# The last batch's row scatters bound to other steps of the routing

## The chip, the cores and the metric

The kernel runs on one core of a Trainium2 chip. The metric is the device time of one execution in microseconds. The reader needs these engines: TensorE (PE, matrix products; PEld is its weight load), VectorE (DVE), ScalarE (ACT), GpSimd (POOL) and SyncE (SP). DMAs are issued by SP and, where rows go to computed places ("indirect" DMAs), by POOL; all of them run on the core's 16 DMA engines. An instruction starts when its engine has reached it and every semaphore it waits for has its value.

## The reference, cut to what matters

Four batches of 512 tokens with 256 features go through two layers. Each layer is an attention followed by a mixture of experts, and everything is float32. The change touches only the experts of the second layer:

```python
logits = xf @ Wg                                   # 8 experts
top_vals, top_idx = jax.lax.top_k(logits, 2)
gate_score = jax.nn.softmax(top_vals, axis=-1)
comb = jnp.einsum('tke,tk->te', one_hot, gate_score) * alpha
for e in range(8):
    hdn = _layernorm(xf, ln_w[e], ln_b[e])
    a = jax.nn.gelu(hdn @ fc1_w[e] + fc1_b[e], approximate=True)
    y = a @ fc2_w[e] + fc2_b[e]
    out = out + y * comb[:, e:e + 1]
```

Each of the 2048 tokens needs only two of the eight experts, so the kernel sorts the tokens by expert and computes only those products.

## The kernel before, in words

**Sorting by scatter.** `route_steps` handles one batch of 512 tokens: it normalizes, computes the logits, picks two experts for each token and counts places. The result is `rt_posi` (line 931), the row in the DRAM buffer `rows` for each of a token's two copies. Eight indirect DMAs on POOL per batch (line 951, 128 rows of 258 floats each) write the normalized tokens from `rowbuf` to those places. They are put into a list, `pending`. `scatter_pending(n, behind)` takes the next n from that list and records them; if `behind` is given, the DMA also waits for that instruction. The reason given in the code is that the DMAs are to come a few at a time beside the other work.

**The last batch.** Its routing cannot lie beside attention, since attention is over by then. `layer1_attention` ends with a loop over `PIECES` in which the steps of this routing alternate with pieces of four expert tiles that were started ahead (`y_ahead`, `hp_ahead`; two tiles each of experts 0 and 1, whose rows were already there). The order in this stretch is:

- the places of the last batch, `rt_posi`; the first two of its eight scatters follow without any other wait;
- `tile_table` on DVE (lines 1009 to 1068): from the counts it works out for each of 39 tiles which expert and which rows it has. Its first large step is a comparison that makes `tt_past` (line 1025); the table that SP reads is `tab`, whose third row is finished at line 1047 (`L1.tabled`); `tt_valid` and `tt_aside` follow;
- two additions of the second biases to x (line 998, `L1.biased`), after which the batch's x is written to `out` by SP (line 1000).

In the kernel before, the third and fourth scatter wait for `L1.tabled`, the fifth and sixth for the first bias addition, the seventh and eighth for the second.

**What waits for the scatters.** `layer1_experts` then runs the expert tiles. SP loads the 128 rows of the first three tiles (line 1215, `row<-rows`). The first of these loads waits for all scatters, since a tile's rows may come from any of them. PE turns a tile's rows (line 1120, `ht`), multiplies with the first weights (line 1145, `hp`) and the second (line 1170, `y`). POOL adds the result to `out` with an accumulating indirect DMA (line 1188), one at a time. Of the four tiles ahead, the fourth's `y_ahead` stands behind the first tile's `ht` in PE's order.

**What sets the order.** PE's order and, among the experts, SP's order are written out by hand. DVE, ACT and POOL are ordered by a scheduler. Its order of DVE, ACT and POOL instructions, and the order on PE and SP, are the same in both kernels; only waits of POOL instructions differ.

Of the kernel before, what the change touches and what calls it, by code (L numbers as in the profile page):

```python
# [13 lines left out]
ALU = mybir.AluOpType  # L14
# [21 lines left out]
TILES = NB * S * 2 // P + EX - 1  # L36
GROUP = 32
RING = 3
# [25 lines left out]
def two_layers(ctx: ExitStack, tc: tile.TileContext, io, out):  # L64
    nc = tc.nc
# [616 lines left out]
    def layer1_attention(sts):  # L682

        units = []
        for b in range(NB):
            units += [(b, t, n) for t in range(NT) for n in range(NC)]
        ps, aTs = {}, {}
        routes, queries = {}, None  # L690
        kvs = mha_kvs(sts, (NB - 1,))
        done = None
        for i in range(len(units) + 4):
            if i < len(units):
                b, t, n = units[i]
                ps[i] = mha_scores(sts[b], n, t)
                unit = sts[b]
                if i + 1 < len(units) and units[i + 1][0] > 0 and units[i + 1][2] == 0:
                    bias = mha_bias(sts[units[i + 1][0]], units[i + 1][1])
                    after(bias, done, "a piece to a unit")  # L700
                done = sts[b]["unit"]
            if i < 3:
                next(kvs)
            if 0 <= i - 2 < len(units):
                b, t, n = units[i - 2]
                turns = mha_turns(sts[b], n, t, ps[i - 2][0])
                aTs[i - 2] = next(turns)
                next(turns)
            if 11 <= i < 15:
                next(kvs)  # L710
            if 0 <= i - 4 < len(units):
                b, t, n = units[i - 4]
                if n == NC - 1:
                    added = mha_out(sts[b], t)
            if 0 <= i - 3 < len(units):
                b, t, n = units[i - 3]
                mha_values(sts[b], n, t, aTs.pop(i - 3), ps.pop(i - 3)[1])
            for route in routes.values():
                next(route, None)
            if pending and (i < len(units) or i % 2 == 1):  # L720
                scatter_pending(2, unit["unit"] if i < len(units) else added)
            if i == 2:
                next(kvs)
            if queries:
                next(queries, None)
            if 0 <= i - 2 < len(units):
                next(turns)
            b = i // (2 * NT) + 1
            if b < NB and i % (2 * NT) == QUERIES:
                queries = mha_q_pieces(b, sts)  # L730
            if i == len(units) - 5:
                slots = slots_ahead()
            if i == len(units) - 3:
                held = []
                tiles = tiles_ahead(slots, *load_ahead(), sts[NB - 1]["unit"], held)
            if i == len(units) + 2:
                next(tiles)
            b, k = divmod(i - 11, 2 * NT)
            if k == 0 and 0 <= b < NB:
                routes[b] = route_steps(L1, b)  # L740
                next(routes[b])
        scatter_pending(2, L1.normed)
        for n in PIECES:
            for _ in range(n):
                next(tiles, None)
            for route in routes.values():
                next(route, None)
            if len(L1.run) < NB:
                scatter_pending(2, L1.turned)
            if len(L1.run) == NB and L1.table is None:  # L750
                L1.table = tile_table(L1)
                scatter_pending(2, L1.tabled)
        for i in L1.biased:
            scatter_pending(2, i)
        for _ in range(LEFT):
            next(tiles)

        for add in held:
            add()
        held.clear()  # L760
        return slots, tiles, held
# [53 lines left out]
    L1 = Layer(1, EX, FF1 // P, ET0, None)  # L815
# [188 lines left out]
    def tile_table(L):  # L1004

        lim = L.run[NB - 1][:, 0:EX]
        big_shape = [P, TILES, EX]
        n = tsmall([P, EX], "tt_n")
        i = nc.vector.tensor_tensor(n, lim, base[:, 0:EX], ALU.subtract)
        after(i, L.placed, "the rows' places first")  # L1010
        if L.done is not None:
            nc.vector.tensor_tensor(n, n, L.done[:, 0:EX], ALU.subtract)
        nc.vector.tensor_scalar(n, n, float(P - 1), None, ALU.add)
        n_i = tsmall([P, EX], "tt_ni", I32)
        nc.vector.tensor_copy(n_i, n)
        nc.vector.tensor_scalar(n_i, n_i, 7, None, ALU.logical_shift_right)
        nt = tsmall([P, EX], "tt_nt")
        nc.vector.tensor_copy(nt, n_i)

        c = tsmall([P, EX], "tt_c")  # L1020
        nc.vector.tensor_copy(c[:, 0:1], nt[:, 0:1])
        for e in range(1, EX):
            nc.vector.tensor_tensor(c[:, e : e + 1], c[:, e - 1 : e], nt[:, e : e + 1], ALU.add)
        past = t4(big_shape, f"tt_past{L.n}")
        nc.vector.tensor_tensor(
            past, c.unsqueeze(1).to_broadcast(big_shape), tile_f.unsqueeze(2).to_broadcast(big_shape), ALU.is_le
        )
        ef = const.tile([P, TILES], F32, tag="tt_ef", name=f"tt_ef{L.n}")
        nc.vector.tensor_reduce(ef, past, AX.X, ALU.add)
        nc.vector.tensor_scalar(ef, ef, float(EX - 1), None, ALU.min)  # L1030
        step = tsmall([P, EX], "tt_step")
        nc.vector.tensor_scalar(step, nt, float(-P), float(REGION), ALU.mult, ALU.add)
        if L.done is not None:
            nc.vector.tensor_tensor(step, step, L.done[:, 0:EX], ALU.subtract)
            nc.vector.tensor_tensor(step, step, L.done[:, 1:], ALU.add)
        tmp = t4(big_shape, f"tt_tmp{L.n}")
        nc.vector.tensor_tensor(tmp, past, step.unsqueeze(1).to_broadcast(big_shape), ALU.mult)
        off = const.tile([P, TILES], F32, tag="tt_off", name=f"tt_off{L.n}")
        nc.vector.tensor_reduce(off, tmp, AX.X, ALU.add)
        nc.vector.scalar_tensor_tensor(off, tile_f, float(P), off, ALU.mult, ALU.add)  # L1040
        if L.done is not None:
            nc.vector.tensor_scalar(off, off, L.done[:, 0:1], None, ALU.add)
        tab = const.tile([P, 3, TILES], I32, tag="tab", name=f"tab{L.n}")
        nc.vector.tensor_copy(tab[:, 0, :], ef)
        nc.vector.tensor_scalar(tab[:, 1, :], off, float(EX * REGION - P), None, ALU.min)
        nc.vector.tensor_tensor(tab[:, 2, 0:RING], ef[:, 0:RING], L.held, ALU.not_equal)
        L.tabled = nc.vector.tensor_tensor(tab[:, 2, RING:], ef[:, RING:], ef[:, 0 : TILES - RING], ALU.not_equal)

        dl = tsmall([P, EX], "tt_dl")
        i = nc.vector.tensor_tensor(dl[:, 0 : EX - 1], lim[:, 1:], lim[:, 0 : EX - 1], ALU.subtract)  # L1050
        after(i, L.placed, "the rows' places first")
        i = nc.vector.tensor_scalar(dl[:, EX - 1 :], lim[:, EX - 1 :], -1.0, None, ALU.mult)
        after(i, L.placed, "the rows' places first")
        nc.vector.tensor_tensor(tmp, past, dl.unsqueeze(1).to_broadcast(big_shape), ALU.mult)
        left = const.tile([P, TILES], F32, tag="tt_left", name=f"tt_left{L.n}")
        nc.vector.tensor_reduce(left, tmp, AX.X, ALU.add)
        nc.vector.tensor_tensor(left, left, off, ALU.subtract)
        nc.vector.tensor_scalar(left, left, lim[:, 0:1], None, ALU.add)
        valid = const.tile([P, TILES], F32, tag="tt_valid", name=f"tt_valid{L.n}")
        nc.vector.tensor_scalar(valid, left, token[:, 0:1], None, ALU.is_gt)  # L1060
        aside = const.tile([P, TILES], F32, tag="tt_aside", name=f"tt_aside{L.n}")
        if L.n == 0:
            past_ys = float(2 * NB * S)
            nc.vector.tensor_scalar(aside, valid, -past_ys, past_ys, ALU.mult, ALU.add)
        else:
            nc.vector.tensor_scalar(aside, valid, spare_neg, spare, ALU.mult, ALU.add)
        total = const.tile([1, 1], I32, tag="tt_total", name=f"tt_total{L.n}")
        nc.vector.tensor_copy(total, c[0:1, EX - 1 :])
        return tab, valid, aside, total
# [408 lines left out]
```

## Time and profile before

| | |
|---|---|
| three runs, us | 915.99, 918.59, 918.94 (median 918.59) |
| profiled execution, us | 917.38 |
| its span, us | 915.6 |
| granted TensorE clock | 0.996 of full |
| PE busy | 868.2 us (95%) |
| DVE busy | 426.1 us (47%) |
| ACT busy | 334.2 us (36%) |
| POOL busy | 226.2 us (25%) |
| scatters (line 951) | 64, min 967 ns, median 973, max 1394 |
| mean DMA rate | 155 GB/s |

The span is the time between the first and last recorded instruction; 1.78 us of the profiled execution lie outside it. Busy times are sums over the whole span. A POOL span of an indirect DMA is the time in which POOL works on the instruction, not the time in which the data move. In the timeline a line has the start and the duration in us, the engine, the source line, the operation with its output and inputs, and in brackets how long the engine sat idle before and what it waited for. "SPq" is SP's issue of a DMA. Starts are in us from the beginning of the span.

### The profile page before, as it was taken

How to read it: one execution, taken by the hardware profiler on the slowest of the kernel's cores; microseconds unless marked ns; L12 is line 12 of the kernel's file. 1: busy time of each engine (PE TensorE's matmuls, PEld its weight loads, DVE VectorE, ACT ScalarE, POOL GpSimd, SP SyncE). 2: the span in 40 equal slices, each digit the busy share in tenths (PEclk: the TensorE clock that was granted, in tenths of full speed). 3: DMA queues.
4: the chain of work that ended last, by engine and by line, in shares of the span. 5: the costliest groups of instructions: out<-in, count | busy, mean ns of one | idle time of the engine just before them, and what ended most of it. 6: DMA issues, size and time to landing. Idle time of an engine off the chain costs nothing.

```text
span 915.6 us, 15375 instructions
## 1 busy us (share of the span) xinstructions
PE 868.2 (95%) x5578; PEld 659.9 (72%) x5578; DVE 426.1 (47%) x1253; ACT 334.2 (36%) x749; POOL 226.2 (25%) x276
## 2 busy tenths in 40 slices
PE   6899999998999998999999999999989999999995
PEld 2456464755699996556676666667879999999995
DVE  5646473736623331765675686676721111111120
ACT  4323331222211111475574565565512333222231
POOL 2303014044313222000130250351642122122122
PEclk9999999999999999999999999999999999999999
DMA  8999933030188893600000123221257956877961
GB/s 309 293 261 245 246 134 112 15 101 35 54 276 262 252 347 116 229 24 1 24 2 1 46 69 119 71 70 56 74 158 247 304 168 193 262 238 239 322 213 22
DMA packets 55028, 142.08 MB, mean 155 GB/s; under 512 B 6894, under 2 KB 32933, under 8 KB 48800
## 3 DMA queue, kind: packets, MB, share of 16 engines
q1 hardware_dynamic: 39264, 102.89, 33.5%
q0 software_dynamic: 15392, 38.10, 16.4%
q8 instruction: 48, 0.79, 0.3%
q14 instruction: 36, 0.29, 0.1%
q10 hardware_dynamic: 288, 0.00, 0.0%
HBM read 131.52 MB, written 39.91 MB: 187 GB/s over the span
## 4 chain that ended last, share of the span: by engine, by line
PE 43%; DVE 7%; issue 4%; ACT 4%; DMA 2%; POOL 0%; SPq 0%; POOLq 0%; ACTq 0%; DVEq 0%
PE hp L1145 12%; PE y L1170 11%; PE s L616 5%; PE a2t L639 4%; PE o L664 4%; ACT p L629 2%; DVE p L625 2%; PE q L600 1%; ACT a2T L644 1%; PE hp_ahead L1145 1%; PE ht L1120 1%; PE wo L679 1%; DMA ys<-yw,to 1%; PE o L670 1%; DMA yb<-ys 1%
## 5 line engine op out<-in xcount | busy, mean ns | idle before, releaser
L1154 ACT ACTIVATE aT<-hp,w1s 128x128 f32<-128x128 f32 x248 | 67.3, 382 | 163.3 <-issue 153.2
L1145 PEld LDWEIGHTS hp<-hT,w1s 128*128 128x128 f32 x992 | 115.8, 192 | 2.4 <-DVE hT L1126 0.8
L1145 PE MATMUL hp<-hT,w1s 128*128 128x128 f32 x992 | 116.1, 275 | 0.6 <-DVE hT L1126 0.6
L1170 PE MATMUL y<-w2s,aT 128*128 128x256 f32 x496 | 112.3, 379 | 0.5 <-ACT aT L1154 0.5
L1170 PEld LDWEIGHTS y<-w2s,aT 128*128 128x128 f32 x496 | 91.8, 190 | 11.9 <-ACT aT L1154 0.7
L629 ACT ACTIVATE p<-p,s_nm 128x1024 f32<-128x1024 f32 x64 | 73.5, 1148 | 73.3 <-DVE s_nm L625 73.2
L625 DVE CUSTOM_DVE_ANT_0 p<-s,mbias 128x1024 f32<-128x1024 f32 x64 | 75.7, 1221 | 38.7 <-PE s L616 38.6
L1188 POOL DMA_INDIRECT out<-yw,to x31 | 47.8, 1541 | 168.1 <-DMA out<-yw,to 59.6
L1174 DVE TENSOR_SCALAR yw<-y,row 128x256 f32<-128x256 f32 x59 | 28.6, 484 | 122.3 <-PE y L1170 122.3
L951 POOL DMA_INDIRECT rows<-rowbuf,rt_posi x64 | 64.2, 1004 | 81.8 <-DVE rt_posi L931 25.4
L639 PEld LDWEIGHTS a2t<-ident,p 128*128 128x128 f32 x512 | 56.2, 142 | 36.8 <-issue 21.7
L639 PE MATMUL a2t<-ident,p 128*128 128x128 f32 x512 | 70.8, 278 | 5.7 <-DVE xn2T L594 2.6
L616 PE MATMUL s<-kT,q2T 64*128 64x512 f32 x256 | 65.1, 615 | 0.7 <-DVE s_nm L625 0.7
L664 PE MATMUL o<-a2T,v 128*64 128x128 f32 x1024 | 63.3, 276 | 0.1
L315 PE MATMUL s<-ctxT,q0T 128*128 128x512 f32 x128 | 62.4, 634 | 0.7 <-ACT q0T L292 0.7
L664 PEld LDWEIGHTS o<-a2T,v 128*64 128x64 f32 x1024 | 55.4, 137 | 8.5 <-issue 6.8
L644 ACT COPY a2T<-a2t 128x512 f32<-128x512 f32 x96 | 53.3, 582 | 16.1 <-PE a2t L639 16.1
L1126 DVE TENSOR_SCALAR hT<-ht,w1s 128x128 f32<-128x128 f32 x62 | 22.6, 406 | 77.3 <-PE ht L1120 71.2
L345 PE MATMUL hq<-a0T,ctxn 128*128 128x512 f32 x128 | 56.8, 596 | 0.1
L1145 PEld LDWEIGHTS hp<-hT,w0s 128*128 128x128 f32 x448 | 54.3, 192 | 3.2 <-DVE hT L1122 1.8
L1145 PE MATMUL hp<-hT,w0s 128*128 128x128 f32 x448 | 55.0, 276 | 1.0 <-DVE hT L1122 1.0
L1170 PE MATMUL y<-w0s,aT 128*128 128x256 f32 x224 | 53.1, 380 | 0.7 <-ACT aT L1150 0.7
(258 smaller groups left out, 1206.8 us busy)
## 6 DMA issues: line engine op xcount, KB each, us to landing
w1s<-in_w1p SPq DMA_DIRECT2D x34, 1030.0 KB
w2s<-in_w2p SPq DMA_DIRECT2D x34, 1024.0 KB
rows<-zeros POOLq DMA_DIRECT2D x8, 2064.0 KB
w0s<-in_w1p SPq DMA_DIRECT2D x31, 512.0 KB
w0s<-in_w2p SPq DMA_DIRECT2D x31, 512.0 KB
row<-rows SPq DMA_DIRECT2D x59, 129.0 KB
ctxT<-in_ctxT SPq DMA_DIRECT2D x4, 1024.0 KB
ctxn<-in_ctx SPq DMA_DIRECT2D x4, 1024.0 KB
```

The costliest lines, as they stand in the source:

```text
L315: nc.tensor.matmul(sp[:, h, :], st["qT"][:, c, bass.ts(t, P)], ctxT[b][:, c, bass.ts(h, 512)], start=(c == 0), stop=(c == NC - 1),)
L345: nc.tensor.matmul(op, ctxn[b][:, j, bass.ts(c, P)], aT[:, j, :], start=(j == 0), stop=(j == NJ - 1))
L616: nc.tensor.matmul(sps[r][:, k, :], st["qT"][at, n, bass.ts(t, P)], st["kT"][at, n, bass.ts(k, 512)], start=True, stop=True,)
L625: nc.vector.tensor_tensor_reduce(p, sps[r].rearrange("p h n -> p (h n)"), st["mbias"][:, t, :], -ATT_SCALE, -ATT_SCALE * LEAST, ALU.add, A ...
L629: nc.scalar.activation(p, p, AF.Exp, bias=nm, scale=-1.0, accum_out=tot[:, r : r + 1])
L639: nc.tensor.transpose(pt[:, bass.ts(j, P)], p[:, bass.ts(4 * g + j, P)], ident)
L644: nc.scalar.copy(d, pt)
L664: nc.tensor.matmul(op[r * HD : r * HD + HD, :], st["v"][:, j, bass.ts(2 * n + r, HD)], aT[:, r, bass.ts(j, P)], start=(j == 0), stop=(j == ...
L951: i = nc.gpsimd.indirect_dma_start(out=rows[:, :], out_offset=bass.IndirectOffsetOnAxis(ap=pos_i[:, k, t : t + 1], axis=0), in_=buf[:, k, ...
L1145: nc.tensor.matmul(o, w1[:, c * ff + f * P : c * ff + f * P + P], hT[:, c, :], start=(c == 0), stop=(c == NC - 1),)
L1154: nc.scalar.activation(aT[:, f, :], hp[:, f // 4, bass.ts(f % 4, P)], AF.Gelu_apprx_tanh, bias=w1[:, at : at + 1])
L1170: nc.tensor.matmul(op, aT[:, f, :], w2[:, f * D : f * D + D], start=(f == 0), stop=(f == nf - 1))
```

## The change

The third and fourth scatter of the last batch now wait for the comparison that makes `tt_past`, the fifth and sixth for the end of `tab`, the seventh and eighth for the first bias addition. The first two are as they were. No instruction is added, removed or put elsewhere in an engine's order. The diff:

```diff
@@ layer1_attention @@
             if len(L1.run) == NB and L1.table is None:
                 L1.table = tile_table(L1)
-                scatter_pending(2, L1.tabled)
-        for i in L1.biased:
-            scatter_pending(2, i)
+                for i in L1.tabled:
+                    scatter_pending(2, i)
+        scatter_pending(2, L1.biased[0])
         for _ in range(LEFT):
             next(tiles)
@@ tile_table @@
         past = t4(big_shape, f"tt_past{L.n}")
-        nc.vector.tensor_tensor(
+        begun = nc.vector.tensor_tensor(
             past, c.unsqueeze(1).to_broadcast(big_shape), tile_f.unsqueeze(2).to_broadcast(big_shape), ALU.is_le
         )
@@
-        L.tabled = nc.vector.tensor_tensor(tab[:, 2, RING:], ef[:, RING:], ef[:, 0 : TILES - RING], ALU.not_equal)
+        done = nc.vector.tensor_tensor(tab[:, 2, RING:], ef[:, RING:], ef[:, 0 : TILES - RING], ALU.not_equal)
+        L.tabled = begun, done
```

## The prediction

> **What bounds the kernel now.** I read the page's busy times first: PE is busy in 868.2 of 915.6 us, so a change that touches no product can gain only where PE stands still. Then I read the waits of PE from 675 us to the end, to see what the experts' stage loses: there are three, `ht` on the DMA of `row` (2.6 us, once), `hp` on DVE's `hT` (0.6) and the last `y` on ACT (0.5). After the first of these the chain of waits consists of PE's `hp`, `ht` and `y` alone up to 887 us. So there is one gap that this change can reach, and what fills it comes off the end. The timeline around it:
>
> ```profile
> 657.80 0.16 DVE L931 CAST rt_posi<-rt_pos 128x8 int32<-128x8 f32 x1
> ...
> 658.74 0.97 POOL L951 DMA_INDIRECT rows<-rowbuf,rt_posi  x1 [2.09 <-issue]
> ...
> 660.01 0.97 POOL L951 DMA_INDIRECT rows<-rowbuf,rt_posi  x1 [0.30 <-DVE tt_step L1034]
> ...
> 661.01 0.48 DVE L1025 TENSOR_TENSOR tt_past<-tt_c,tile_f 128x312 f32<-128x312 f32 x1
> ...
> 663.38 0.19 DVE L1047 TENSOR_TENSOR tab<-tt_ef 128x36 int32<-128x36 f32 x1
> ...
> 664.35 0.97 POOL L951 DMA_INDIRECT rows<-rowbuf,rt_posi  x1 [3.36 <-issue]
> ...
> 665.62 0.97 POOL L951 DMA_INDIRECT rows<-rowbuf,rt_posi  x1 [0.30 <-DVE tt_left L1058]
> 665.75 0.68 DVE L998 TENSOR_TENSOR x<-b,x 128x512 f32<-128x512 f32 x1
> ...
> 667.21 0.97 POOL L951 DMA_INDIRECT rows<-rowbuf,rt_posi  x1 [0.61 <-issue]
> ...
> 668.48 0.97 POOL L951 DMA_INDIRECT rows<-rowbuf,rt_posi  x1 [0.30 <-issue]
> 669.76 0.97 POOL L951 DMA_INDIRECT rows<-rowbuf,rt_posi  x1 [0.30 <-issue]
> ...
> 671.03 0.97 POOL L951 DMA_INDIRECT rows<-rowbuf,rt_posi  x1 [0.30 <-issue]
> ...
> 674.41 2.13 SPq L1215 DMA_DIRECT2D row<-rows  x3
> ...
> 676.38 0.44 PE L1120 MATMUL ht<-ident,row 128*128 128x128 f32 x2 [2.58 <-DMA row<-rows]
> ```
>
> Eight scatters, each 0.97 us long, follow each other at 1.27 us where nothing holds them. POOL stands idle for 3.36 us before the third and 0.61 before the fifth. The eighth starts at 671.03; SP, which has waited for it 5.1 us by its own list of waits, issues the first row load 3.38 us later; PE starts `ht` 1.97 us after that. PE's last product ahead of `ht` starts at 670.19 and lasts 3.62, so PE is free at 673.81: it waits 2.58 us for rows. That makes the scatters' end the wait that ends last here.
>
> **The new starts.** Three scatters of before give the time from the end of the DVE step that is waited for to the scatter: 657.96 to 658.74, 663.57 to 664.35 and 666.43 to 667.21, each 0.78 us. With this and the pitch of 1.27:
> - First and second: 658.74 and 660.01, as now.
> - Third: the comparison at line 1025 ends at 661.49, plus 0.78 is 662.27. Fourth: 663.54.
> - Fifth: line 1047 ends at 663.57, which would allow 664.35, but POOL is free only at 664.81. Sixth: 666.08.
> - Seventh: the first bias addition ends at 666.43, which would allow 667.21; POOL gives 667.35. Eighth: 668.62.
>
> So the eighth starts 671.03 - 668.62 = 2.41 us earlier. Only the first of the three waits binds: from the third on the scatters are back to back. The same lags of 3.38 and 1.97 us put the row load at 672.00 and the rows at 673.97, 0.16 us after PE is free. Of the gap of 2.58 us 2.41 go, and late next is PE itself, whose end at 673.81 caps the gain at 2.58.
>
> **What takes some of it back.** The batch's x (512 KB) is written to `out` from 667.34 on, and in the table of stretches the DMA engines are full in 669 to 670:
>
> ```profile
> 668.00:669.00 1.00, 1.00 (x12) 1.00 (x11) 0.00 (x0) 0.00 (x0) 0.70 (x2) 1.00 0.69 245
> 669.00:670.00 1.00, 1.00 (x12) 1.00 (x11) 0.00 (x0) 0.00 (x0) 0.69 (x2) 1.00 1.02 346
> 670.00:671.00 1.00, 1.00 (x8) 0.92 (x7) 0.00 (x0) 0.00 (x0) 0.73 (x1) 1.00 0.60 198
> 671.00:672.00 1.00, 1.00 (x7) 0.87 (x6) 0.00 (x0) 0.38 (x2) 0.96 (x1) 1.00 0.37 132
> ```
>
> The last two columns are the DMA engines' share and the rate in GB/s. A scatter alone moves 132 KB at 132 GB/s and a share of 0.37, as the last one did. Now the last one's data fall into the full microsecond. Its delay is at least nothing (the engines have room again from 670) and at most about the half microsecond in which the write of x uses what is left of the engines; I take 0.2, nearer to nothing, because before the sixth scatter ran through the same stretch and the seventh and eighth were not held up. Net gain 2.4 - 0.2 = **2.2 us**.
>
> **What else moves, at no cost.** Behind the scatters in POOL's queue stands only the first addition to `out` (672.31 before, 669.9 at the earliest now); it must also wait for the write of x, and the next additions follow it one by one. Nobody waits for them soon: POOL is idle for 8.8 us before the fourth. If this addition meets the row loads, it did so before. SP runs its table reads and weight loads behind the row loads, so these come 2.4 us earlier with PE. The tile that needs new weights (its loads were issued at 681.09 and 681.78, the DMA engines then full to 689) has its `hT` ready at 691.65 for an `hp` at 692.07: 0.4 us of room. As PE and SP both move with the rows, that room stays; should it go, it costs some tenths. The last 30 us (branch, last tile, last addition) follow PE and move as a whole.
>
> [...] The third to sixth scatter now run while DVE is fully busy (busy 2.60 of 2.60 us from 662.20 on) with the table, where before POOL was idle. [...] The row first: all 64 scatters of this trace last between 967 and 1394 ns. The best row is the same table in the first layer, beside eight scatters back to back:
>
> ```profile
> 238.53 0.98 POOL L951 DMA_INDIRECT rows<-rowbuf,rt_posi  x1 [0.30 <-issue]
> 239.81 0.97 POOL L951 DMA_INDIRECT rows<-rowbuf,rt_posi  x1 [0.30 <-issue]
> 241.09 0.97 POOL L951 DMA_INDIRECT rows<-rowbuf,rt_posi  x1 [0.30 <-issue]
> ```
>
> There the comparison, its reductions and products last 0.47 to 0.48 us each, as they do without scatters in the second layer. Neither engine holds the other up, so by the rows the price is nothing. [...]
>
> **Sum.** The profiled execution took 917.38 us: a span of 915.6 and 1.78 around it. 917.38 - 2.2 = **915.2**. The three runs' median is 918.59, from which the same gain would give 916.4. About 0.3% (2.75 us) is what a measurement of this kernel can tell from no change: my gain is 0.24% and its cap 0.28%, so it lies just inside that bound, and the runs' own spread of 2.95 us decides on which side it is read.
>
> **The rivals.**
> 1. *The gain stands, at its full size or a bit more.* The row loads come at the cap of 2.58 us or the downstream loads fall better: 914.8, and against the median of the runs shown over 0.3%. For it: the gap's size and PE as the only bound after it. Against: the tenths lost to the write of x.
> 2. *Hidden anyway.* The rows come earlier, but another wait ends at the same place: the row loads meet the first addition to `out`, or the weights of the tile at 692 come late. Price 1.5 to 2.5 us of the gain, leaving about 917. For it: the full DMA engines from 682 to 689 and the 0.4 us of room. Against: both loads move with PE.
> [...]
> 4. *The change doesn't do what it says*, if POOL waits for later DVE steps than named. The waits are counts of DVE's instructions, and the three lags of 0.78 us show that such a wait is released by the step named. I give it little, within the second case.
>
> **How the numbers follow.** My forecast of 915.2 (own range 914.8 to 915.7) has 0.54, the first rival 0.15, the second with the fourth 0.14, the third with the page's price 0.17. Half of the forecast's weight, less a little, and nearly all of the first rival's are read as more than 0.3% faster: 0.42. The rest of the forecast and the second give 0.40 for no change. The slower cases, most of which lie over 0.3%, and a little for what I do not see give 0.18. The range of 912.8 to 919.5 holds forecast, first and second rival with the runs' spread around them, and leaves out most of the third.
>
> **What would show it.** Right: scatters 3 to 8 of the last batch back to back at 1.27 us, the last 2.4 us nearer to `rt_posi`; their duration still 0.97; table steps of 0.48 us; SP's wait for the scatters shorter by 2.2 to 2.4 us; PE's wait before the first `ht` down from 2.58 to 0.4 us or less. Wrong: scatters longer than 1.4 us, gaps in DVE's table, `hp_ahead` later than 8.7 us after `rt_posi`, a row load that lands later than 2 us after its issue, or a new wait of `hp` after 676 us.

## The result, and the profile after

The changed kernel takes **915.10 us** (median of 20 runs, 913.38 to 917.41) against 917.68 us (20 runs, 915.82 to 919.77) of the kernel before, taken in turn on the same chip. The ratio is 0.9976, with a 95% interval of 0.9969 to 0.9983: 2.2 us faster by the ratio, 2.6 by the medians. The profiled execution took 914.52 us with a span of 912.7 and a mean granted clock of 0.993 (before 917.38, 915.6 and 0.996).

The timeline of the changed kernel around the change. Lines from 1048 on carry a number one higher than before:

```profile
656.10 0.17 DVE L931 CAST rt_posi<-rt_pos 128x8 int32<-128x8 f32 x1
...
657.03 0.97 POOL L951 DMA_INDIRECT rows<-rowbuf,rt_posi  x1 [2.10 <-issue]
658.30 0.98 POOL L951 DMA_INDIRECT rows<-rowbuf,rt_posi  x1 [0.30 <-DVE tt_c L1023]
...
659.31 0.48 DVE L1025 TENSOR_TENSOR tt_past<-tt_c,tile_f 128x312 f32<-128x312 f32 x1
...
660.57 0.98 POOL L951 DMA_INDIRECT rows<-rowbuf,rt_posi  x1 [1.28 <-issue]
...
661.85 1.25 POOL L951 DMA_INDIRECT rows<-rowbuf,rt_posi  x1 [0.30 <-DVE tt_off L1040]
...
662.17 0.24 DVE L1042 TENSOR_SCALAR tt_off<-tt_off,done 128x39 f32<-128x39 f32 x1
...
662.71 0.40 DVE L1045 TENSOR_SCALAR tab<-tt_off 128x39 int32<-128x39 f32 x1
...
663.41 0.97 POOL L951 DMA_INDIRECT rows<-rowbuf,rt_posi  x1 [0.30 <-DVE tt_left L1058]
...
664.68 0.97 POOL L951 DMA_INDIRECT rows<-rowbuf,rt_posi  x1 [0.31 <-issue]
...
664.81 5.47 PE L1146 MATMUL hp_ahead<-hT_ahead,w1s 128*128 128x128 f32 x32
...
665.96 0.97 POOL L951 DMA_INDIRECT rows<-rowbuf,rt_posi  x1 [0.30 <-issue]
667.24 0.97 POOL L951 DMA_INDIRECT rows<-rowbuf,rt_posi  x1 [0.30 <-issue]
...
670.12 3.62 PE L1171 MATMUL y_ahead<-w2s,aT_ahead 128*128 128x256 f32 x16
...
670.51 2.33 SPq L1216 DMA_DIRECT2D row<-rows  x3
...
673.57 0.38 PE L1121 MATMUL ht<-ident,row 128*128 128x128 f32 x2
```

The two profiles are best laid over each other at the start of `rt_posi` (657.80 before, 656.10 after):

| us after `rt_posi` starts | before | after | moved |
|---|---|---|---|
| third scatter | 6.55 | 4.47 | 2.08 earlier |
| eighth scatter | 13.23 | 11.14 | 2.09 earlier |
| first row load issued | 16.61 | 14.41 | 2.20 earlier |
| `hp_ahead` starts | 8.71 | 8.71 | 0 |
| PE starts `ht` | 18.58 | 17.47 | 1.11 earlier |

PE starts `ht` without a wait; the list of PE's waits from 650 to 900 us, in which before had 2.6 us for `row`, now begins with these (total, times, longest):

```profile
PE hp L1146 <- DVE hT L1127: 0.6, 1, 0.6
PE y L1171 <- ACT aT L1155: 0.5, 1, 0.5
PE b L994 <- DVE yw_ahead L1175: 0.2, 1, 0.2
```

So of the 2.86 us between the two profiled executions, 1.11 arise in the stretch of the change. Another 1.70 is the distance between the two `rt_posi`; nothing is changed ahead of it, and it is already there at 380 us. That part is scatter between executions. The 1.11 are fewer than the 2.20 that the rows gained, because `hp_ahead` took 5.47 us in place of 3.84. The table of stretches of the changed kernel says why. Its columns are the length of the slice, the busy time and the instructions of PE, PEld, DVE, ACT and POOL, then the granted PE clock, the DMA engines' share and GB/s:

```profile
665.00:666.00 1.00, 1.00 (x6) 1.00 (x6) 0.61 (x1) 0.00 (x0) 0.69 (x2) 0.50 0.30 103
666.00:667.00 1.00, 1.00 (x7) 1.00 (x7) 0.00 (x0) 0.00 (x0) 0.94 (x1) 0.50 0.74 243
667.00:668.00 1.00, 1.00 (x6) 1.00 (x6) 0.00 (x0) 0.00 (x0) 0.76 (x1) 0.50 0.99 345
668.00:669.00 1.00, 1.00 (x10) 1.00 (x8) 0.00 (x0) 0.00 (x0) 0.21 (x1) 0.80 0.74 250
669.00:670.00 1.00, 1.00 (x11) 1.00 (x10) 0.00 (x0) 0.00 (x0) 0.39 (x1) 1.00 0.24 83
```

The reader is to see the clock column at 0.50 for three slices, with six or seven products a microsecond where the last slice, at full clock, has eleven. No such stretch was in the profile of before at this place, so the first question was whether the change made it.

### The profile page after: what moved, and what is told of

Its sections match the earlier page's. It is cut to its first block, busy times and chain, and to the rows that moved or that the text cites. A ratio compares the mean times of both kernels' runs of the same rounds, so it can differ in the third digit from the quotient of the medians.

```text
span 912.7 us, 15375 instructions
## 1 busy us (share of the span) xinstructions
PE 868.7 (95%) x5578; PEld 662.3 (73%) x5578; DVE 426.4 (47%) x1253; ACT 334.3 (37%) x749; POOL 226.4 (25%) x276
## 4 chain that ended last, share of the span: by engine, by line
PE 45%; DVE 6%; ACT 4%; issue 4%; POOL 0%; ACTq 0%; POOLq 0%; DVEq 0%
PE hp L1146 12%; PE y L1171 11%; PE s L616 5%; PE a2t L639 4%; PE o L664 4%; ACT p L629 2%; DVE p L625 2%; PE hp_ahead L1146 1%; PE q L600 1%; PE v L510 1%; ACT a2T L644 1%; PE k L496 1%; PE y_ahead L1171 1%; PE ht L1121 1%; PE wo L679 1%
```

## The experiments

The kernels ran in three sets; those of a set and their runs of before share a chip. "Clock" is the mean over a kernel's runs of each run's mean granted TensorE clock.

| kernel | set | runs | median, us | ratio to before [95%] | clock |
|---|---|---|---|---|---|
| before again | 1 | 22 | 917.67 | 1.0002 [0.9994, 1.001] | 0.9927 |
| after again | 1 | 6 | 914.81 | 0.9961 [0.9945, 0.9976] | 0.9948 |
| no waits | 1 | 6 | 921.42 | 1.004 [1.0026, 1.0055] | 0.9905 |
| all late | 1 | 6 | 922.48 | 1.0051 [1.0035, 1.0067] | 0.9907 |
| first wait undone | 2 | 22 | 916.44 | 0.9988 [0.9977, 0.9999] | 0.9935 |
| first wait alone | 2 | 14 | 916.91 | 1.0006 [0.9991, 1.002] | 0.9935 |
| six at `tt_past` | 2 | 18 | 914.17 | 0.9967 [0.9956, 0.9978] | 0.9949 |
| four at once | 2 | 6 | 912.27 | 0.9946 [0.9927, 0.9965] | 0.9963 |
| after, third time | 3 | 12 | 915.24 | 0.9984 [0.9969, 0.9998] | 0.9947 |
| four at once again | 3 | 12 | 919.55 | 1.003 [1.0014, 1.0046] | 0.9922 |
| six at once | 3 | 8 | 920.53 | 1.0034 [1.0015, 1.0053] | 0.9916 |
| four, then at `tt_past` | 3 | 6 | 921.16 | 1.0058 [1.0039, 1.0078] | 0.9915 |

The runs of before had medians of 917.39, 916.89 and 916.69 us and clocks of 0.9929, 0.9936 and 0.9940 in the three sets. The ratio is not the quotient of the two medians; the two differ by up to 0.0011 ("after again" has 0.9972 by its medians), which is not small against the effects here. In every experiment each engine's instructions stand in the order of the changed kernel; only waits of scatters differ.

### Both kernels once more

No edit. Before:

> The kernel before, unchanged, to see each run's mean granted TensorE clock. In the profile of the changed kernel that clock was halved for 3.8 us within the stretch of the change (665 to 668.8), and its runs show mean clocks of 0.992 to 0.995. Theory A (the halving has nothing to do with the change; the old gap of 2.58 us hid its 1.6 us): the runs of before show the same mix, most at 0.993 to 0.994 and some at 0.995 to 0.996, and time does not depend on which. Theory B (the change brings the halving about): before is at 0.995 to 0.996 in all runs. Median 917.7 us, ratio 1.000 within 0.001.

After:

> The changed kernel, unchanged, on the same chip. Both theories: 915.2 us, ratio 0.9975. Theory A: runs at the higher clock are faster than those at the lower one by 1.1 to 1.3 us, since PE's end now decides when the first tile's rows are turned. In the profile the eighth scatter starts 11.1 us after the places (13.2 before).

The gain repeats (0.9961), and the profile of the changed kernel has the slow `hp_ahead` again (5.47 us, clock at 0.5 from 666.0 to 669.4). But the profile of before has a slow stretch too, in another place, in PE's timeline right behind the gap:

```profile
676.34 0.69 PE L1120 MATMUL ht<-ident,row 128*128 128x128 f32 x2 [2.90 <-DMA row<-rows]
676.82 4.79 PE L1170 MATMUL y_ahead<-w2s,aT_ahead 128*128 128x256 f32 x16
```

`y_ahead` took 4.79 us where it took 3.62 in the first profile of before: the clock was halved from 675.8 to 679.2. Half-clock stretches thus come without the change too, in some executions and not in others of the same kernel. This one costs 1.2 us (4.79 - 3.62), the one in `hp_ahead` 1.6 (5.47 - 3.84); each is 3.4 us long, not the 3.8 that the expectation read.

### All later

```diff
-                for i in L1.tabled:
-                    scatter_pending(2, i)
-        scatter_pending(2, L1.biased[0])
+        scatter_pending(6, L1.biased[1])
```

> The last six scatters wait for the second bias addition: the third starts at 10.3 us after the places, the eighth at 16.6, which is 3.4 us later than before. Theory (each microsecond of the last scatter is one of the end while PE waits): 917.7 + 3.4 = 921.1 us, ratio 1.0037, and PE's wait for the first rows 6.0 us, or 4.4 with the halved clock, at the same time. Rival (the gap was not what set the end): ratio below 1.002.

The sign and the size of the lever are confirmed: the eighth scatter starts 16.69 us after `rt_posi`, 3.46 later than before, and PE's wait in the timeline grows to 4.52:

```profile
679.75 0.69 PE L1119 MATMUL ht<-ident,row 128*128 128x128 f32 x2 [4.52 <-DMA row<-rows]
680.23 5.55 PE L1169 MATMUL y_ahead<-w2s,aT_ahead 128*128 128x256 f32 x16
```

The ratio (1.0051) is above the expected 1.0037: `y_ahead` pays 1.93 us more behind the longer gap, with the clock at a half from 677.3 to 684.1. This run also answers the question about `hp_ahead`. Its scatters come later than before, and `hp_ahead` still takes 5.47 us, with the clock at a half from 667.1 to 670.5: the slow `hp_ahead` does not need earlier scatters. PE's long wait hides that loss here.

### Which of the three waits carries the gain

The first wait undone, the other two as changed:

```diff
-                for i in L1.tabled:
-                    scatter_pending(2, i)
+                scatter_pending(2, L1.tabled[1])
+                scatter_pending(2, L1.tabled[1])
         scatter_pending(2, L1.biased[0])
```

> Only the first of the three moved waits is undone: the third to sixth scatter wait for the end of the table as the third and fourth did before, the seventh and eighth for the first bias addition. Theory (only the first of the three moved waits binds; the gain is the rows' lead): the third scatter starts 6.55 us after rt_posi, the eighth 5 x 1.27 = 6.36 later, at 12.9 after rt_posi (before 13.23, after 11.14), so the row load comes only about 0.3 us earlier than before, PE keeps a wait of about 2.3 us before the first ht, and the time is about 0.3 us under before: ratio 0.9997, within 0.999 to 1.0005. Rival (the later two waits carry the gain, or the time moves for another reason than the rows' lead): 914.8 to 916, ratio about 0.997 to 0.998.

The first wait alone, the other two as before:

```diff
-                for i in L1.tabled:
-                    scatter_pending(2, i)
-        scatter_pending(2, L1.biased[0])
+                scatter_pending(2, L1.tabled[0])
+        for i in L1.biased:
+            scatter_pending(2, i)
```

> Only the first of the three moved waits: third and fourth wait for the table's first comparison, fifth and sixth for the first bias addition, seventh and eighth for the second, as before. Theory: third at 4.47 us after rt_posi, fourth 1.27 later, but the fifth still waits for the first bias addition, 9.41 after rt_posi, and the last three follow at 1.27: the eighth at 13.23, as before, so no gain: ratio 1.000 within 0.999 to 1.001, with PE's wait before ht still about 2.6 us. Rival (two scatters fewer beside the bias additions and the write of x are worth something by themselves): up to 1 us faster.

All six at the first comparison:

```diff
-                for i in L1.tabled:
-                    scatter_pending(2, i)
-        scatter_pending(2, L1.biased[0])
+                for n in (2, 4):
+                    scatter_pending(n, L1.tabled[0])
```

> All six remaining scatters wait only for the table's first comparison; the waits for the table's end and the first bias addition are gone. Theory: those two waits do not bind in the changed kernel, so the scatters start at the same times (third 4.47 us after rt_posi, eighth 11.14) and the time is that of the changed kernel, ratio to before 0.997 within 0.996 to 0.9985. Rival (the harm of the kernel without any wait, late semaphore updates of PE, comes from scatters that wait for nothing but their queue): slower, 918 to 922, with the second product of the second biases more than 2 us late.

With the first wait undone the eighth scatter starts 12.95 us after `rt_posi`, as expected. The ratio of 0.9988 lies just below the expected range, though its interval holds the expected 0.9997 (the medians give 0.9995). The row load came 0.9 us earlier rather than 0.3, since the lag behind the last scatter was 2.79 us this time and not 3.38. That lead did not reach PE: from the row load's issue to `ht` it took 2.87 us and not 1.97, and `ht` starts 18.61 us after `rt_posi`, as in the kernel before (18.58). PE's wait before `ht` was 1.00 and not 2.3, because this execution too had `hp_ahead` at half clock (5.37 us). This one stands as compatible rather than as a confirmation: it speaks against the full gain without the first wait, and leaves 0.1 to 2.1 us. With the first wait alone, the timeline of that kernel shows where the lead is lost:

```profile
661.05 1.26 POOL L951 DMA_INDIRECT rows<-rowbuf,rt_posi  x1 [0.30 <-DVE tt_off L1040]
...
664.71 0.97 POOL L951 DMA_INDIRECT rows<-rowbuf,rt_posi  x1 [2.40 <-issue]
...
674.17 0.44 PE L1121 MATMUL ht<-ident,row 128*128 128x128 f32 x2 [1.22 <-DMA row<-rows]
```

The fourth scatter is early, POOL then stands for 2.40 us, the eighth is back at 13.23, and the time is that of before (1.0006). (The wait of 1.22 is again shorter than 2.6 by a slow `hp_ahead`, 5.47 us.) With all six at `tt_past` the scatters start at the changed kernel's times (third 4.47, eighth 11.14) and the gain is the changed kernel's (0.9967). In the changed kernel, then, only the wait for `tt_past` binds; but the other two had to move with it, or they would have bound in its place. This profile also has no half-clock stretch here, so that it shows the change's effect by itself:

```profile
665.12 3.84 PE L1146 MATMUL hp_ahead<-hT_ahead,w1s 128*128 128x128 f32 x32
...
668.80 3.62 PE L1171 MATMUL y_ahead<-w2s,aT_ahead 128*128 128x256 f32 x16
...
670.67 2.55 SPq L1216 DMA_DIRECT2D row<-rows  x3
...
672.66 0.44 PE L1121 MATMUL ht<-ident,row 128*128 128x128 f32 x2 [0.24 <-DMA row<-rows]
```

`ht` starts 16.25 us after `rt_posi` (656.41 here), 2.33 earlier than before, and waits 0.24 us for its rows.

### Can the scatters go earlier still?

First without any wait:

```diff
-                for i in L1.tabled:
-                    scatter_pending(2, i)
-        scatter_pending(2, L1.biased[0])
+                scatter_pending(6)
```

> All eight scatters follow the places at once. The last starts 0.94 + 7 x 1.27 = 9.8 us after the places, 1.3 us earlier than in the changed kernel, the row load at about 13.1, the rows at 15.1. Theory of the cap (PE's own work ends the stretch at 16.0 us after the places, or 17.6 with the halved clock): no more than 0.2 us faster than the changed kernel, 914.9 to 915.2 us. Rival without a cap: another 1.3 us, 913.8. [...]

The scatters ran back to back at 0.97 us, the eighth 9.95 us after `rt_posi`, and still the kernel was slower than before (1.004). Neither expectation had the reason. Its timeline (line numbers two lower):

```profile
667.92 0.48 DVE L1173 TENSOR_SCALAR yw_ahead<-y_ahead,row_ahead 128x256 f32<-128x256 f32 x1 [3.78 <-remote]
...
668.46 2.07 PE L992 MATMUL b<-fc2b,combT 8*128 8x256 f32 x4 [4.07 <-issue]
```

DVE stands still for 3.78 us before `yw_ahead`. Its input, PE's `y_ahead`, ends at 663.34 by the trace, but the semaphore updates of its products are recorded from 661.33 to 667.83 and not with the products' ends, as in the changed kernel (0.01 us behind them). The last arrives as the last scatter ends (667.83). PE's next product waits for DVE, the clock is halved from 665.7 to 676.0, and the early rows are worth nothing.

Then third and fourth alone without a wait, in two sets:

```diff
-                for i in L1.tabled:
-                    scatter_pending(2, i)
+                scatter_pending(2)
+                scatter_pending(2, L1.tabled[1])
         scatter_pending(2, L1.biased[0])
```

> Third and fourth scatter follow the first two without a wait; fifth to eighth wait as in the changed kernel (table's end, first bias addition). The scatters then start at 0.94, 2.21, 3.48, 4.75, 6.55, 7.82, 9.41 and 10.68 us after rt_posi: the eighth 0.46 us before that of the changed kernel. Theory of the cap: PE's own end (with its half clock) is late by then, so the time is that of the changed kernel, 914.8, ratio to before 0.997. Rival one (what made the kernel without waits slow begins with scatters right behind the places): 918 to 922 with late semaphore updates of PE, the second bias product more than 2 us late. Rival two (it needs the unbroken run of eight, or scatters 5 to 8 beside PE's y_ahead at 3 to 6 us after rt_posi): no harm, as the theory.

> Third and fourth scatter right behind the first two, the rest as in the changed kernel, once more. Theory one (cap): rows come 0.46 us earlier than in the changed kernel, but PE is late next; at an equal clock the same time as the changed kernel or up to 0.5 us less, ratio 0.9965 to 0.9975; its 912.27 of before was a set of six runs with few half-clock stretches. Theory two (it is really better: without a gap of PE, the half-clock stretch in this place comes less often): ratio 0.994 to 0.996 again and a mean clock of 0.996.

The same kernel gave 0.9946 in the second set and 1.003 in the third; no theory had that. The timeline in the second set, and then in the third:

```profile
663.33 0.47 DVE L1175 TENSOR_SCALAR yw_ahead<-y_ahead,row_ahead 128x256 f32<-128x256 f32 x1
...
663.86 1.13 PE L994 MATMUL b<-fc2b,combT 8*128 8x256 f32 x4 [0.17 <-DVE yw_ahead L1175]
```

```profile
663.63 0.48 DVE L1175 TENSOR_SCALAR yw_ahead<-y_ahead,row_ahead 128x256 f32<-128x256 f32 x1 [2.48 <-remote]
...
664.17 2.07 PE L994 MATMUL b<-fc2b,combT 8*128 8x256 f32 x4 [2.75 <-DVE yw_ahead L1175]
```

The late updates are there in the third set (`y_ahead` ends at 660.36, updates are recorded until 663.59) and not in the second, where none of the four profiles has any. The profile of the third set is of an execution of 915.92 us, the second fastest of its twelve, which had reached `rt_posi` 3.9 us sooner than the profile of before for reasons ahead of the change; the slower ones are known by their times alone. Two more kernels of the third set asked whether the length of the unbroken run decides. Six at once:

```diff
-                for i in L1.tabled:
-                    scatter_pending(2, i)
+                scatter_pending(4)
         scatter_pending(2, L1.biased[0])
```

> Third to sixth scatter right behind the first two, the last two wait for the first bias addition: scatters at 0.94 to 7.3 after rt_posi without a break, then 9.41 and 10.68. If scatters five and six beside PE's y_ahead (3 to 7 us after rt_posi) hold up PE's semaphore updates: slow as the kernel without waits, 920 to 922, second bias product late by more than 2 us. If it needs the run of all eight: as with four at once, ratio 0.994 to 0.9975.

Four at once, then four at `tt_past`:

```diff
-                for i in L1.tabled:
-                    scatter_pending(2, i)
-        scatter_pending(2, L1.biased[0])
+                scatter_pending(2)
+                scatter_pending(4, L1.tabled[0])
```

> Third and fourth right behind the first two, fifth to eighth wait for the table's first comparison, which lets them go at 4.47 us after rt_posi, when the fourth has just ended (about 5.7): an unbroken run of eight, in the same places as in the kernel without waits (0.94 to 9.9 after rt_posi). If the harm there comes from the unbroken run in this place: 920 to 922 again with late semaphore updates of PE. If it comes from scatters queued without a wait of their own: as with four at once, ratio 0.994 to 0.9975.

Both are slow (1.0034 and 1.0058), DVE's wait before `yw_ahead` is 2.62 and 5.34 us, and the last updates are recorded at 668.52 and 668.40, 1.4 and 1.6 us after the last scatter of the run. So it makes no difference whether a scatter has a wait of its own. Where the updates are late, a run of six beside `y_ahead` is enough, and eight make the wait longer (2.48 and 2.62 us with six, 3.78 and 5.34 with eight). Beside them, as the control:

> The changed kernel once more, beside the next three on the same chip. Ratio to before 0.9975, within 0.996 to 0.9985; mean granted clock between that of before (0.9927 to 0.9936 in two sets of runs) and 0.995.

The changed kernel kept a gain there (0.9984), smaller than in the other sets. Its profile shows some late updates, by up to about 0.4 us if matched in their order, but they have caught up by 662.15, before the end of `y_ahead`, and `yw_ahead` waits for nothing. **The changed kernel is the version to keep**: four at once beat it in one set only, and the kernels that start scatters right behind the places lose 2.8 to 5.3 us in the two sets whose profiles have late updates (ratios of 1.003 to 1.0058 by 917).

## Why the prediction was right, step by step

**The lever: right.** Forecast 915.2, measured 915.10; the ratio times the profiled 917.38 us is 915.18. That the two agree to 0.1 us is in part luck: the forecast started from one execution, 0.3 us under the median of before (917.68), and the medians differ by 2.6 us and not by 2.2. PE's wait before `ht` fell from 2.58 to nothing (0.24 and 0.32 in the profiles without a half-clock stretch), and the time followed the eighth scatter in both directions: earlier by 2.09, 0.9976; the same, 1.0006; later by 3.46, 1.0051. A lead of only 0.28 gave 0.9988, with an interval that reaches 0.9999.

**"Only the first of the three waits binds": right**, shown by the six at `tt_past`. The third scatter starts 4.47 us after `rt_posi`, as worked out (662.27 - 657.80).

**"Back to back at 1.27": right but for one term.** The fourth scatter took 1.25 us and not 0.97, so the eighth came 2.09 us earlier and not 2.41. The sum took 0.97 from the first layer's rows, but the table there has no line 1042: the code takes that step in the second layer only. In the five profiles in which that step of 0.24 us starts about 0.32 us into a scatter (the changed kernel's three and the two with the first wait alone or all six at `tt_past`), this scatter takes 1.25 to 1.26 us; no other scatter of the last batch takes more than 1.07, in any profile. No run moved the step alone, so that it is the cause is argued, not shown.

**"0.2 given back to the write of x": not seen.** The row load was issued 3.27 us behind the eighth scatter against 3.38 before, so that the rows gained 2.20. In the other profiles without a long wait for `yw_ahead` this lag lies between 2.79 and 3.50, and 0.2 is too small to be told from that. The net of 2.2 came out right by luck, by two misses of 0.3 each that cancel (0.32 on the scatters; 0.2 to be lost and 0.11 won on the lag). SP's own wait for the scatters, which was to be shorter by 2.2 to 2.4, went from 5.1 to 3.4 only: this mark missed.

**"PE's own end, at 673.81, caps it": right as the next limit, but not fixed.** The sum took `hp_ahead` at 3.84 us. In an execution whose clock halves there it takes 5.47; PE is then free 17.47 us after `rt_posi`, and half of the gain shows. In the kernel before, the wait for rows would hide the same loss, as it did with all late. That the medians still differ by the forecast has two sides: the kernel before has its own half-clock stretches behind its gap (in one of its two profiles), and the changed kernel's mean clock was not the lower one in either set that has both. Over all runs, fitted with one level for each kernel and set, 0.001 of mean clock goes with 0.58 us. At an equal clock of 0.995 before stands at 916.2 to 916.5 and after at 914.3, 914.3 and 914.9, which is 1.3 to 2.2 us; most of the rest in the first set goes with its higher clock (0.9948 against 0.9929, 1.1 us by this slope). Whether the missing gap makes stretches rarer isn't settled: in the third set the clocks differ by only 0.0007.

**"Neither engine holds the other up": nearly.** The large table steps stay at 0.47 to 0.48 us. But line 1045 took 0.40 us (0.17 before) and ended at 663.11, with the fourth scatter (663.10); `tt_valid` took 0.50 (0.24 before) and ended at 664.39, with the fifth (664.38). Some small steps, then, last until the scatter's end, a quarter of a microsecond longer each; others, such as line 1042 within the fourth scatter (0.24 us), do not, but may hold it, as said above. What makes them end together no run shows. A row of before showed it already, and the prediction did not read it: `tt_step` at line 1032, 128x8 elements, took 0.38 us and ended at 659.71, where the first scatter ended. The longer DVE steps did not reach PE. The fourth scatter's 0.28 us did: they moved all behind it, and about as much PE still waits for its rows in the two profiles without a half-clock stretch (0.24 and 0.32). The prediction also gives 0.17 to a slower case that puts a price on the scatters beside the table. No run shows that price: the third to sixth scatter took 0.97 to 1.25 us in the changed kernel, the longest of this batch in any profile 1.26, and the eighth came 2.09 us earlier.

**The rivals.** The slower case fell with those rows. The case of a gain hidden downstream fell with PE's waits, which have nothing new after 676 us. A slower outcome with early scatters exists (no waits, 921.42 us), but its loss is DVE's wait of 3.78 us before `yw_ahead`, and such a loss was seen only where scatters begin sooner than the change lets them.

## What to carry to other kernels

When a chain of waits is moved, move all its links: one moved alone gave nothing, since the next bound 2.4 us later. Read the cap of such a gain as a range, not a number: the engine that is late next has its own variation (here `hp_ahead` at 3.84 or 5.47 us), and a wait hides it until it is gone. And do not take the last microsecond by dropping waits altogether without runs on more than one chip or set: what looked best in one (0.9946) was slower than the start in the next (1.003).

## What the runs showed of the hardware that was not expected

**Half-clock stretches in a busy PE.** The stretch in `hp_ahead` lasts from 665.00 to 668.41, 3.41 us; the others named above last 3.4 us too, but for 6.8 in all late behind its gap and about 10 with no waits. The trace does not read as an idle PE: in 660 to 665 PE was recorded 0.82 to 1.00 busy in each microsecond. But the 2.3 us between `y_ahead` and `hp_ahead` hold only the small products of the second biases (8 rows of weights). The table has what PE did in the 3.41 us ahead of three half-clock stretches, and in as long a time ahead of the same two places in the profile of before, where the clock stayed at 1.00. The third column has PE's busy time, the fourth the part of it in products with 128 rows of weights:

| profile, ahead of | from, to, us | PE busy, us | with 128 rows, us | clock behind |
|---|---|---|---|---|
| after, half clock in `hp_ahead` | 661.59 to 665.00 | 3.23 | 1.12 | 0.50 |
| before, `hp_ahead` | 663.10 to 666.51 | 3.23 | 1.13 | 1.00 |
| before again, half clock at its gap | 672.36 to 675.77 | 1.08 | 1.08 | 0.50 |
| all late, half clock at its gap | 673.89 to 677.30 | 1.33 | 1.33 | 0.50 |
| before, `ht` behind its gap | 672.97 to 676.38 | 0.84 | 0.84 | 1.00 |

Neither column sorts these rows: the two places ahead of `hp_ahead` are alike, and the gap that no half clock followed holds the least. What these rows show is that such stretches come behind the second biases and behind the gap in some executions and not in others; what decides between them is not shown, and no run moved these products.

**Late semaphore updates of PE.** Beside runs of scatters, the updates of PE's products were recorded up to 6.1 us after the products' ends (four, then at `tt_past`: 668.40 for 662.29). They appeared in two of three sets, in the kernel before as well (there behind 671 us, where nobody waited for them). What holds them up stays open: the scatters go with it in every profile where it cost time, but the same scatters had none in the second set. The ends of products are modelled, so that products which really ended late can't be excluded. The kept traces add a rival: the nine profiles of before and of the first and third set hold 7515 to 7702 semaphore updates, the five others, which have no late one here, 8665 to 8671. Where updates come late, then, a part of them is missing from the record as well, and what thins the record, or the recording itself, may be what delays them. No experiment took these apart.
